# Turning a conv output to tokens by channels: four TensorE transposes per tile, or VectorE's 32x32 block transposes and a trip through DRAM

## The chip, the cores and the metric

The kernel runs on one core of one Trainium2 chip. The metric is the device time of one execution in microseconds (us), the median of several runs. Engines are named as the profile names them: PE (TensorE, the matrix engine; PEld is its weight load), DVE (VectorE), ACT (ScalarE), POOL (GpSimd) and SP (SyncE, which here only issues DMAs; SPq is its queue).

## What is computed

A decoder layer in float32 on 512 tokens (2 batches of 256) of 512 channels: a state-space mixer, a quantised product with a context, and a feed-forward with mixed experts. Nearly all of the time goes to the mixer. Cut to what matters here:

```python
proj = einsum('bsd,od->bso', h, in_proj_w)        # gate (8192), hBC (8192+2048), dt (128)
hBC  = silu(causal_conv(hBC, conv_w, conv_b))     # 4 taps per channel
hid, B, C = split(hBC)                            # hid: 128 heads of 64 channels
hid_dt = hid * dt[..., None]                      # dt: one value per token and head
y = sum over earlier tokens j of (C_i . B_j) * decay(i, j, head) * hid_dt[j]   # plus Dp * hid
y = y * silu(gate)                                # then an RMS norm over groups of 1024 channels
out = einsum('bsd,od->bso', y * rstd * gnorm_w, out_proj_w)
```

The projection makes hid with channels on the partitions (128 channels by 512 tokens), which the convolution wants. The sum over earlier tokens contracts over tokens, so it wants hid with tokens on the partitions, each value multiplied by dt of its token and head. Something has to turn hid round.

## The kernel before

**Tiles and steps.** The 8192 channels are 64 tiles of 128 channels (two heads each), in 8 groups g of 8. The main loop (L975) makes one step per tile, and one more per group for the tile of B and C of the next group ("state"), so 9 steps q = 0 to 8 in a group; the state has q = 4. It is a software pipeline: in one step, `z` is the tile being projected, `z1` the tile of the step before, `z2` the tile before that. On PE, ACT, DVE and POOL the instructions run in the order in which the program writes them; only the order of SP's DMAs is left to the scheduler of the framework, which places each by its own estimate of when it is ready.

**What one step does,** in program order:

- PE `begin(z)`: from group 1 on a product in seven block products instead of eight (L298); four of them come first. SP loads the weights (L342) and the decays of coming tiles (L457); POOL sums weights (L352 to L355).
- ACT starts z1's convolution out of PSUM (L313); then `times_dt(z2)` (L480): eight multiplications, one per block of 128 tokens and head, from PSUM tile `pht` to SBUF tile `hc`; then z1's gate (L427), and two copies out of `begin(z)`'s PSUM (`copy_first`, L386 and L387).
- For each of z1's two heads: DVE scans the decays (L487), ACT multiplies two blocks of them (L491), POOL multiplies by the inner products C.B into `mT` (L497). Between the two heads, DVE adds the other three taps of z1's convolution (L318), ACT takes its silu into `hid` (L321), and DVE combines `begin(z)`'s parts (`sum_begun`, L395 to L398).
- At q = 2 the norm of the group before: PE transposes the sum of squares (L537), DVE reduces it (L539), POOL computes the reciprocal root (L41 to L51) and then sums for the output product (L578 to L606).
- `seventh`: one block product of the output projection of an earlier group (L631), at q = 0, 2, 4, 5, 6, 7 ahead of the heads, at q = 1 behind everything (so "late"). In the last group there is one at q = 8 as well and a whole one at q = 3.
- `finish(pair)`: when two tiles z2 are ready, at q = 1, 3, 5 and 8 (one tile per step in the first group), PE multiplies `mT` by `hc` (`heads`, L508), and `gated` follows: DVE (L520, L523), ACT's square into `sq` (L528) and its scaling into `yw` (L530), POOL's sum of squares (L529).
- PE `complete(z)`: the remaining three block products.
- `by_tokens(z1)`: four PE transposes of `hid` against the identity into PSUM tile `pht` (L469). `times_dt` of the next step reads it.

So a tile's hid leaves the silu in one step, is turned at that step's end, is multiplied by dt at the start of the next step, and meets `heads` in that next step at the earliest. `conv` sums have a tile of their own (tag conv, 2 buffers), `y` has one buffer, `hc` two, `hid` three, the decays `dec` five, the weights `w` four.

Of the kernel before, what the change touches and what calls it, by code (L numbers as in the profile page):

```python
# [7 lines left out]
F32 = mybir.dt.float32  # L8
AF = mybir.ActivationFunctionType
ALU = mybir.AluOpType  # L10
# [3 lines left out]
P = 128  # L14
NB = 2
NT = 4
T = NT * P
S = T // NB
D = 512
KD = D // P  # L20
NG = 8
GJ = 8
HD = 64
# [12 lines left out]
def power(nc, pool, var, n, name):  # L36

    r0 = pool.tile([P, n], F32, tag="rs_r0", name=f"r0_{name}")
    ex = pool.tile([P, n], F32, tag="rs_ex", name=f"ex_{name}")
    nc.gpsimd.memset(ex[:], -0.5)  # L40
    nc.gpsimd.tensor_tensor(r0[:], var, ex[:], ALU.pow)  # L41
    return r0


def newton(engine, pool, out, r0, var, n, name):

    t0 = pool.tile([P, n], F32, tag="rs_t0", name=f"t0_{name}")
    engine.tensor_tensor(t0[:], r0[:], r0[:], ALU.mult)
    engine.tensor_tensor(t0[:], t0[:], var, ALU.mult)
    engine.tensor_scalar(t0[:], t0[:], -0.5, 1.5, ALU.mult, ALU.add)  # L50
    engine.tensor_tensor(out, r0[:], t0[:], ALU.mult)  # L51
# [3 lines left out]
def kernel(  # L55
# [25 lines left out]
    nc = tc.nc  # L81
# [14 lines left out]
    ident = const.tile([P, P], F32, name="ident")  # L96
# [5 lines left out]
    cw = const.tile([P, 80, 4], F32, name="cw")  # L102
    cb = const.tile([P, 80], F32, name="cb")
    ncw = const.tile([P, NG, 4], F32, name="ncw")
    gw = const.tile([P, NG * GJ], F32, name="gw")
# [4 lines left out]
    dt = const.tile([P, NT, P], F32, name="dt")  # L110


    dram = ctx.enter_context(tc.tile_pool(name="scratch", bufs=1, space=bass.MemoryType.DRAM))
# [5 lines left out]
    ps_y = main.enter_context(tc.tile_pool(name="ps_y", bufs=1, space=PSUM))  # L119
    ps_misc = main.enter_context(tc.tile_pool(name="ps_misc", bufs=1, space=PSUM))  # L120
    ps_seed = main.enter_context(tc.tile_pool(name="ps_seed", bufs=1, space=PSUM))
    ps_out = main.enter_context(tc.tile_pool(name="ps_out", bufs=1, space=PSUM))
    pool = main.enter_context(tc.tile_pool(name="main", bufs=2))
# [16 lines left out]

    with ExitStack() as first:
        pro = first.enter_context(tc.tile_pool(name="pro", bufs=1))
        wdt = pool.tile([P, KD, P], F32, tag="conv", name="wdt")
        nc.sync.dma_start(out=wdt[:], in_=in_w[DT0])
        for to, of in ((dtb, dt_bias.rearrange("(h o) -> h o", o=1)), (alog, a_log.rearrange("(h o) -> h o", o=1))):
            nc.sync.dma_start(out=to[:], in_=of)
# [39 lines left out]
        for b in range(NB):  # L186
# [16 lines left out]
        soft0, soft1, soft2 = (  # L203
            wpool.tile([P, 4 * T], F32, tag="wo", name=f"soft_{n}", bufs=3) for n in range(3)
        )
# [8 lines left out]
        nc.vector.tensor_tensor(v, v, u, ALU.subtract)  # L214
        nc.vector.tensor_tensor(dth, v, lg, ALU.add)
        nc.scalar.activation(within, dth, AF.Exp, scale=nega[:])
        zeros = pro.tile([P, P], F32, name="zeros")
        nc.gpsimd.memset(zeros[:], 0.0)
        for b in range(NB):
            nc.vector.tensor_tensor_scan(  # L220
                across[:, b * P : (b + 1) * P],
                within[:, (2 * b + 1) * P : (2 * b + 2) * P],
                zeros[:],
                1.0,
                ALU.mult,
                ALU.add,
            )
# [12 lines left out]
    def residual(n):  # L240

        if n == 0:
            res["var"] = small.tile([P, NT], F32, name="vare", bufs=1)
            nc.vector.tensor_scalar(res["var"][:], mv[:, :, 1], 1e-5, None, ALU.add)
            res["r0"] = power(nc, small, res["var"][:], NT, "l0")
        elif n == 1:
            res["rstd"] = small.tile([P, NT], F32, name="rstd_l0", bufs=1)
            newton(nc.gpsimd, small, res["rstd"][:], res["r0"], res["var"][:], NT, "l0")
        else:
            t = n - 2  # L250
            x1 = pool.tile([P, D], F32, tag="conv", name=f"x1_{t}")
            nc.vector.tensor_scalar(
                x1[:], acc[:, t, :], mv[:, t, 0:1], res["rstd"][:, t : t + 1], ALU.subtract, ALU.mult
            )
            nc.gpsimd.tensor_tensor(acc[:, t, :], acc[:, t, :], x1[:], ALU.add)
# [44 lines left out]
    def by_batch(ap):  # L300
        return ap.rearrange("p (b s) -> p b s", b=NB)

    class Conv:

        def __init__(self, dst, pvs, w, c, name):
            self.dst, self.w = dst, w
            self.a = pool.tile([P, T], F32, tag="conv", name=f"conv_{name}")
            av, n = by_batch(self.a[:]), NB // len(pvs)  # L310
            self.parts = [(av[:, i * n : (i + 1) * n], pv) for i, pv in enumerate(pvs)]
            for a, pv in self.parts:
                nc.scalar.activation(a, pv, AF.Identity, bias=cb[:, c : c + 1], scale=w[:, 3:4])  # L313
# [75 lines left out]
    def sum_begun(z):  # L389


        if not z.plain:
            z.g1 = pool.tile([P, S], F32, tag="g1", name=f"g1_{z.name}")[:]
            u = z.first[:, 0]
            nc.vector.tensor_tensor(u, z.all, u, ALU.subtract)  # L395
            nc.vector.tensor_tensor(z.h1, z.h1, u, ALU.subtract)
            nc.vector.tensor_tensor(z.g1, z.h1, z.first[:, 1], ALU.add)
            nc.vector.tensor_tensor(z.g0, z.g0, u, ALU.subtract)  # L398
# [7 lines left out]
    def start_conv(z):  # L406
        if isinstance(z, Tile):
            z.hid = pool.tile([P, T], F32, tag="hid", name=f"hid_{z.c}", bufs=3)
            z.convs = [Conv(z.hid[:], [by_batch(z.xy[0])], cw[:, z.c], z.c, f"h_{z.c}")]
            return  # L410
        g = z.g
        z.sT = [pool.tile([P, T], F32, tag=f"{n}T", name=f"{n}T_{g}", bufs=1) for n in "bc"]
        z.convs = [Conv(z.sT[0][:], [by_batch(z.xy[0])], cw[:, 64 + g], 64 + g, f"b_{g}")]
        if z.plain:
            pvs, w = [by_batch(z.xy[1])], cw[:, 72 + g]
        else:

            pvs, w = [a.unsqueeze(1) for a in (z.g0, z.g1)], ncw[:, g]
        z.convs.append(Conv(z.sT[1][:], pvs, w, 72 + g, f"c_{g}"))

    def gates(z, half):
        if half == 0:
# [36 lines left out]
            decs.append(dec)  # L459
        return decs  # L460

    def by_tokens(z, bank):

        c = z.c

        ps, tag = ((ps_misc, "misc"), (ps_y, "py"))[bank]
        pht = ps.tile([P, NT, 2, HD], F32, tag=tag, name=f"pht_{c}")
        for t in range(NT):
            nc.tensor.transpose(  # L469
                pht[:, t].rearrange("p h d -> p (h d)"), z.hid[:, t * P : (t + 1) * P], ident[:]  # L470
            )
        z.pht = pht

    def times_dt(z):
        c, pht = z.c, z.pht
        z.hc = pool.tile([P, NT, 2, HD], F32, tag="hc", name=f"hc_{c}", bufs=2)
        for t in range(NT):
            for n in range(2):
                h = 2 * c + n
                nc.scalar.mul(z.hc[:, t, n], pht[:, t, n], dt[:, t, h : h + 1])  # L480

    def decayed(z, n):

# [32 lines left out]
    def gated(z, sqsum, yw):  # L516

        c, hid, gate, py = z.c, z.hid, z.gate, z.py
        y = pool.tile([P, T], F32, tag="y", name=f"y_{c}", bufs=1)
        nc.vector.scalar_tensor_tensor(  # L520
            py[:], hid[:], dsk[:, c : c + 1], py[:], ALU.mult, ALU.add
        )
        nc.vector.tensor_tensor(y[:], py[:], gate[:], ALU.mult)  # L523
        if c % GJ == 0:
            nc.scalar.activation(sqsum[:], y[:], AF.Square)
        else:
            sq = pool.tile([P, T], F32, tag="sq", name=f"sq_{c}", bufs=2)
            nc.scalar.activation(sq[:], y[:], AF.Square)  # L528
            nc.gpsimd.tensor_tensor(sqsum[:], sqsum[:], sq[:], ALU.add)  # L529
        nc.scalar.mul(yw, y[:], gw[:, c : c + 1])  # L530

    def norm(o):

# [271 lines left out]
    rows = [Rows(t) for t in range(NT)]  # L805
# [161 lines left out]
    pair = []  # L967
# [7 lines left out]
    for s, (g, q, z) in enumerate(order):  # L975
        z1, z2 = (order[s - n][2] if s >= n else None for n in (1, 2))
        tile1 = isinstance(z1, Tile)
        c = g * GJ + q - (q > BC) if q != BC or g == NG else None
# [7 lines left out]
        n, part = divmod(s - GJ - 5, GT)  # L986
# [3 lines left out]
            next(part_of_context)  # L990
        if z1:
            start_conv(z1)
        if isinstance(z2, Tile):
            times_dt(z2)
        if tile1:
            gates(z1, 0)
        if z:
# [8 lines left out]
        if z1:  # L1006
            if tile1:
                gates(z1, 1)
            z1.convs[0].finish()
        if z:  # L1010
            sum_begun(z)
        if z1 and not tile1:
            z1.convs[1].finish()
            state = z1
# [47 lines left out]
        if isinstance(z2, Tile):  # L1062
            pair.append(z2)
        done = len(pair) == 2 or len(pair) == 1 and g in (0, NG)
        free = 0
        if done:
            free = 1 - len(pair) % 2 * (1 - pair[0].c % 2)
            finish(pair)
            pair = []
        if z:  # L1070
            complete(z)
        if tile1:
            by_tokens(z1, free)
        if late and next(going[0], True):
            going.pop()
        if 2 <= s < 2 + 2 + NT:
            residual(s - 2)
# [23 lines left out]
    add_out(last_o, 3)  # L1101
    rows[3].stats("l1")
    for t in range(2):
        rows[t].transpose("l1", "hc", 2)
    for t in range(2, NT):
        rows[t].scaled("l1", rsc[:, 0:1])
    for t in range(2, NT):
# [8 lines left out]
    for t in range(2):  # L1116
        rows[t].scaled("l2", None)
    for t in range(2, NT):
        rows[t].transpose("l1", "hc", 2)
    context(2)  # L1120
    add_context(2)
    rows[2].stats("l2")
# [78 lines left out]
```

## Time and profile before

| what | value |
| --- | --- |
| median of 3 runs | 847.02 us (846.75 to 847.85) |
| span of the profiled execution, first to last instruction | 846.3 us |
| busy: PE / PEld | 837.8 us / 651.8 us |
| busy: DVE / ACT / POOL | 628.7 / 478.8 / 656.0 us |
| L469, the transposes on PE: count, mean of one record | 256, 274 ns |
| L480, ACT times dt: count, mean of one record | 512, 332 ns |
| DMA: bytes, packets, share of 16 engines | 116.26 MB, 54953, 41.1% for SP's queue |

The page gives no time of the profiled execution but its span, which is 0.7 us under the median of the runs. A record's mean is from its start to its end; matmuls and ACT instructions overlap the next one, so a row of n of them takes less than n times the mean (four PE transposes take 0.44 us on the chain, eight multiplications of L480 1.75 us). Idle time of an engine is put down to what ended it.

### The profile page before, as it was taken

To read this page: it belongs to the slowest core of one execution; us is meant where nothing else is said; L and a number is where in the kernel's file an instruction comes from. 1 tells how busy PE (TensorE), PEld (TensorE's weight loads), DVE (VectorE), ACT (ScalarE), POOL (GpSimd) and SP (SyncE) were. 2 spreads that over 40 slices of the span, in tenths; PEclk is the share of its full clock that TensorE was granted. 3 is DMA by queue.
4 is the path that set the end of the run, shared out by engine and by line. 5 is a ranking of instruction groups with operands and counts; after the bars stand their busy time and mean duration, and the time that the engine had idled before them with its cause. 6 is when DMAs were issued, how large, how long until landed. Compare 5 with 4: busy or idle time off the path is not lost.

```text
span 846.3 us, 13509 instructions
## 1 busy us (share of the span) xinstructions
PE 837.8 (99%) x4368; PEld 651.8 (77%) x4368; DVE 628.7 (74%) x1031; ACT 478.8 (57%) x1362; POOL 656.0 (78%) x675
## 2 busy tenths in 40 slices
PE   8999999999999999999999999999999999999998
PEld 6444578888888888888888888888888888885453
DVE  5667578788779778787779778788778786885663
ACT  2566576556664666556674666557664565655130
POOL 2156689998799888998799888998799888984210
PEclk9999999999999999999999999999999999999999
DMA  6684434346434363255433463235542473323001
GB/s 175 207 295 131 143 125 134 103 150 217 136 123 136 127 223 125 79 183 177 165 132 110 149 228 113 75 125 155 184 138 72 139 245 98 116 88 124 1 1 50
DMA packets 54953, 116.26 MB, mean 137 GB/s; under 512 B 7746, under 2 KB 8002, under 8 KB 54883
## 3 DMA queue, kind: packets, MB, share of 16 engines
q1 hardware_dynamic: 54882, 115.40, 41.1%
q8 instruction: 35, 0.57, 0.3%
q14 instruction: 36, 0.29, 0.1%
HBM read 111.84 MB, written 3.54 MB: 136 GB/s over the span
## 4 chain that ended last, share of the span: by engine, by line
PE 81%; POOL 11%; ACT 3%; DVE 2%; issue 2%; DMA 1%; SPq 0%; POOLq 0%; DVEq 0%; ACTq 0%
PE x L298 18%; PE m L631 17%; PE y L298 13%; PE py L508 9%; PE x L292 4%; PE y L292 4%; PE po L688 3%; PE pht L469 3%; POOL mT L497 3%; POOL t L593 2%; POOL yw L584 2%; POOL wo L598 2%; PE pf L803 2%; PE pq L803 2%; PE x_bc L298 1%
## 5 line engine op out<-in xcount | busy, mean ns | idle before, releaser
L497 POOL TENSOR_TENSOR mT<-lT,inner 128x768 f32<-128x768 f32 x128 | 232.6, 1819 | 79.0 <-ACT lT L491 78.5
L318 DVE SCALAR_TENSOR_TENSOR conv_h<-x,cw,conv_h 128x510 f32<-128x510 f32 (+2 forms) x192 | 142.7, 743 | 41.4 <-ACT conv_h L313 36.5
L631 PE MATMUL m<-wo,yw 128*128 128x256 f32 x672 | 155.1, 381 | 0.6
L487 DVE TENSOR_TENSOR_SCAN lT<-dec,seed 128x512 f32<-128x512 f32 x128 | 154.2, 1210 | 0.0
L631 PEld LDWEIGHTS m<-wo,yw 128*128 128x128 f32 x672 | 125.1, 190 | 20.0 <-POOL wo L598 4.3
L491 ACT ACTIVATE lT<-dec,lT 128x128 f32<-128x128 f32 x256 | 90.3, 408 | 86.7 <-DVE lT L487 85.1
L480 ACT ACTIVATE hc<-pht,dt 128x64 f32<-128x64 f32 x512 | 111.6, 332 | 10.9 <-PE pht L469 10.9
L298 PE MATMUL x<-hT,w 128*128 128x256 f32 x440 | 116.6, 387 | 0.0
L298 PE MATMUL y<-hs,w 128*128 128x256 f32 x440 | 112.0, 379 | 0.0
L529 POOL TENSOR_TENSOR sqsum<-sqsum,sq 128x512 f32<-128x512 f32 x56 | 73.1, 1305 | 29.3 <-ACT sq L528 26.5
L298 PEld LDWEIGHTS x<-hT,w 128*128 128x128 f32 x440 | 80.5, 190 | 16.7 <-issue 5.0
L508 PE MATMUL py<-mT,hc 128*64 128x256 f32 (+1 forms) x1024 | 91.2, 329 | 0.6 <-ACT inner L449 0.6
L508 PEld LDWEIGHTS py<-mT,hc 128*64 128x64 f32 x1024 | 64.3, 137 | 31.7 <-issue 9.1
L298 PEld LDWEIGHTS y<-hs,w 128*128 128x128 f32 x440 | 80.3, 190 | 9.2
L528 ACT ACTIVATE sq<-y 128x512 f32<-128x512 f32 x56 | 35.4, 632 | 65.9 <-DVE y L523 65.9
L520 DVE SCALAR_TENSOR_TENSOR py<-hid,dsk,py 128x512 f32<-128x512 f32 x64 | 47.6, 743 | 27.8 <-PE py L508 27.8
L395 DVE TENSOR_TENSOR first<-y,first 128x256 f32<-128x256 f32 x55 | 23.3, 424 | 52.9 <-ACT first L387 52.0
L313 ACT ACTIVATE conv_h<-x,cb,cw 128x512 f32<-128x512 f32 x64 | 49.2, 769 | 18.8 <-PE x L298 18.8
L523 DVE TENSOR_TENSOR y<-py,gate 128x512 f32<-128x512 f32 x64 | 44.3, 692 | 19.4 <-ACT yw L530 18.2
L298 PE MATMUL y<-hs,ws 128*128 128x256 f32 x220 | 56.5, 379 | 0.0
L298 PE MATMUL x<-hT,ws 128*128 128x256 f32 x220 | 56.5, 379 | 0.0
L298 PE MATMUL x<-hs,ws 128*128 128x256 f32 x220 | 56.5, 379 | 0.0
(239 smaller groups left out, 1465.2 us busy)
## 6 DMA issues: line engine op xcount, KB each, us to landing
dec<-decays SPq DMA_DIRECT2D x128, 384.0 KB, 3.5
w<-in_in_w SPq DMA_DIRECT2D x128, 256.0 KB, 3.1
wo<-in_out_w SPq DMA_DIRECT2D x16, 1024.0 KB, 7.2
w_bc<-in_in_w SPq DMA_DIRECT2D x16, 256.0 KB, 5.2
kvin<-in_ctx_kv SPq DMA_DIRECT2D x4, 512.0 KB, 4.7
kvq<-kvin SPq DMA_DIRECT2D x4, 512.0 KB, 2.8
kv<-kvq SPq DMA_DIRECT2D x4, 512.0 KB, 3.5
acc<-in_x SPq DMA_DIRECT2D x4, 256.0 KB, 3.9
```

What stands on the lines that cost most here:

```text
L292: nc.tensor.matmul(pp, w[:, k, :], hT[:, k, :], start=(k == 0), stop=(k == KD - 1))
L298: nc.tensor.matmul(out, w[:, k, :], h[:, k, :], start=clear and k == 0, stop=(k == KD // 2 - 1), skip_group_check=True)
L313: nc.scalar.activation(a, pv, AF.Identity, bias=cb[:, c : c + 1], scale=w[:, 3:4])
L318: nc.vector.scalar_tensor_tensor(a[:, :, d:], pv[:, :, : S - d], self.w[:, 3 - d : 4 - d], a[:, :, d:], ALU.mult, ALU.add)
L480: nc.scalar.mul(z.hc[:, t, n], pht[:, t, n], dt[:, t, h : h + 1])
L487: nc.vector.tensor_tensor_scan(lT[:, 0:NT, :].rearrange("p t i -> p (t i)"), dec[:, 0:T], seed[:], 0.0, ALU.mult, ALU.add)
L491: nc.scalar.mul(lT[:, NT + b, :], dec[:, T + b * P : T + (b + 1) * P], lT[:, 2 * b, P - 1 : P])
L497: nc.gpsimd.tensor_tensor(m[:], z.lT[n][:], inner[:], ALU.mult)
L508: nc.tensor.matmul(z.py[n * HD : (n + 1) * HD, b * S + s * P : (b + 1) * S], z.hc[:, 2 * b + s, n, :], z.mT[n][:, part, :], start=(s == 0) ...
L520: nc.vector.scalar_tensor_tensor(py[:], hid[:], dsk[:, c : c + 1], py[:], ALU.mult, ALU.add)
L529: nc.gpsimd.tensor_tensor(sqsum[:], sqsum[:], sq[:], ALU.add)
L631: nc.tensor.matmul(o.po[:, t, :], lhs[k][:, t * P : (t + 1) * P], rhs[k], start=(k == 0), stop=(k == GJ // 2 - 1))
```

## The change

`by_tokens` no longer uses PE. DVE transposes hid within blocks of 32 by 32 into an SBUF tile `blocks`; SP writes its four partition quarters to a DRAM scratch tile `swap`, each block to its turned place, in pieces of 32 floats (128 bytes), and then reads the scratch back into `hc` with tokens on the partitions, in pieces of 128 floats. `times_dt` multiplies `hc` in place, SBUF to SBUF. `by_tokens` moves from the end of the step to just behind `sum_begun`, `times_dt` from ahead of the gate to behind the silu of z1. The convolution's sums are made in `hid` itself (for the state in a `hid` and a `conv` buffer), `y` is squared in place after its scaling, and buffer counts follow: `hc` 3, `y` 2, `conv` 1, no `sq`. The 128x128 zeros of the prologue become a slice of another tile.

```diff
-            z.convs = [Conv(z.hid[:], [by_batch(z.xy[0])], cw[:, z.c], z.c, f"h_{z.c}")]
+            z.convs = [Conv(z.hid[:], [by_batch(z.xy[0])], cw[:, z.c], z.c, z.hid)]
...
+        sums = [pool.tile([P, T], F32, tag=n, name=f"{n}_bc_{g}", bufs=b) for n, b in (("hid", 3), ("conv", 1))]
...
-    def by_tokens(z, bank):
-        ps, tag = ((ps_misc, "misc"), (ps_y, "py"))[bank]
-        pht = ps.tile([P, NT, 2, HD], F32, tag=tag, name=f"pht_{c}")
-        for t in range(NT):
-            nc.tensor.transpose(
-                pht[:, t].rearrange("p h d -> p (h d)"), z.hid[:, t * P : (t + 1) * P], ident[:]
-            )
-        z.pht = pht
+    def by_tokens(z):
+        blocks = pool.tile([P, NT * 4, 32], F32, tag="blocks", name=f"blocks_{z.c}", bufs=1)
+        nc.vector.transpose(blocks[:].rearrange("p k c -> p (k c)"), z.hid[:])
+        swap = dram.tile([NT, P, P], F32, tag="swap", name=f"swap_{z.c}", bufs=3)
+        to = swap[:].rearrange("t (b r) (a c) -> a r (t b) c", r=32, c=32)
+        for a in range(4):
+            nc.sync.dma_start(out=to[a], in_=blocks[32 * a : 32 * a + 32])
+        z.hc = pool.tile([P, NT, 2, HD], F32, tag="hc", name=f"hc_{z.c}", bufs=3)
+        nc.sync.dma_start(
+            out=z.hc[:].rearrange("p t h d -> p t (h d)"), in_=swap[:].rearrange("t p c -> p t c")
+        )
 
     def times_dt(z):
...
-                nc.scalar.mul(z.hc[:, t, n], pht[:, t, n], dt[:, t, h : h + 1])
+                nc.scalar.mul(z.hc[:, t, n], z.hc[:, t, n], dt[:, t, h : h + 1])
...
-        y = pool.tile([P, T], F32, tag="y", name=f"y_{c}", bufs=1)
+        y = pool.tile([P, T], F32, tag="y", name=f"y_{c}", bufs=2)
...
+        nc.scalar.mul(yw, y[:], gw[:, c : c + 1])
         if c % GJ == 0:
             nc.scalar.activation(sqsum[:], y[:], AF.Square)
         else:
-            sq = pool.tile([P, T], F32, tag="sq", name=f"sq_{c}", bufs=2)
-            nc.scalar.activation(sq[:], y[:], AF.Square)
-            nc.gpsimd.tensor_tensor(sqsum[:], sqsum[:], sq[:], ALU.add)
-        nc.scalar.mul(yw, y[:], gw[:, c : c + 1])
+            nc.scalar.activation(y[:], y[:], AF.Square)
+            nc.gpsimd.tensor_tensor(sqsum[:], sqsum[:], y[:], ALU.add)
...
         if z1:
             start_conv(z1)
-        if isinstance(z2, Tile):
-            times_dt(z2)
         if tile1:
             gates(z1, 0)
...
             z1.convs[0].finish()
+        if isinstance(z2, Tile):
+            times_dt(z2)
         if z:
             sum_begun(z)
+        if tile1:
+            by_tokens(z1)
...
-        if tile1:
-            by_tokens(z1, free)
```

More of the change, by code (lines that the diff above doesn't have):

```diff
@@ L142 @@
         pro = first.enter_context(tc.tile_pool(name="pro", bufs=1))
-        wdt = pool.tile([P, KD, P], F32, tag="conv", name="wdt")
+        wdt = pool.tile([P, KD, P], F32, tag="conv", name="wdt", bufs=1)
         nc.sync.dma_start(out=wdt[:], in_=in_w[DT0])
@@ L216 @@
         nc.scalar.activation(within, dth, AF.Exp, scale=nega[:])
-        zeros = pro.tile([P, P], F32, name="zeros")
-        nc.gpsimd.memset(zeros[:], 0.0)
+        zeros = soft2[:, T : T + P]
+        nc.gpsimd.memset(zeros, 0.0)
         for b in range(NB):
@@ L222 @@
                 within[:, (2 * b + 1) * P : (2 * b + 2) * P],
-                zeros[:],
+                zeros,
                 1.0,
@@ L250, in residual @@
             t = n - 2
-            x1 = pool.tile([P, D], F32, tag="conv", name=f"x1_{t}")
+            x1 = pool.tile([P, D], F32, tag="conv", name=f"x1_{t}", bufs=1)
             nc.vector.tensor_scalar(
@@ L303, with __init__ @@
     class Conv:
-        def __init__(self, dst, pvs, w, c, name):
-            self.dst, self.w = dst, w
-            self.a = pool.tile([P, T], F32, tag="conv", name=f"conv_{name}")
+        def __init__(self, dst, pvs, w, c, a):
+            self.dst, self.w, self.a = dst, w, a
             av, n = by_batch(self.a[:]), NB // len(pvs)
@@ L412, in start_conv @@
         z.sT = [pool.tile([P, T], F32, tag=f"{n}T", name=f"{n}T_{g}", bufs=1) for n in "bc"]
-        z.convs = [Conv(z.sT[0][:], [by_batch(z.xy[0])], cw[:, 64 + g], 64 + g, f"b_{g}")]
+        sums = [pool.tile([P, T], F32, tag=n, name=f"{n}_bc_{g}", bufs=b) for n, b in (("hid", 3), ("conv", 1))]
+        z.convs = [Conv(z.sT[0][:], [by_batch(z.xy[0])], cw[:, 64 + g], 64 + g, sums[0])]
         if z.plain:
@@ L418, in start_conv @@
             pvs, w = [a.unsqueeze(1) for a in (z.g0, z.g1)], ncw[:, g]
-        z.convs.append(Conv(z.sT[1][:], pvs, w, 72 + g, f"c_{g}"))
+        z.convs.append(Conv(z.sT[1][:], pvs, w, 72 + g, sums[1]))
     def gates(z, half):
@@ L460, in load_decays @@
         return decs
-    def by_tokens(z, bank):
-        c = z.c
-        ps, tag = ((ps_misc, "misc"), (ps_y, "py"))[bank]
-        pht = ps.tile([P, NT, 2, HD], F32, tag=tag, name=f"pht_{c}")
-        for t in range(NT):
-            nc.tensor.transpose(
-                pht[:, t].rearrange("p h d -> p (h d)"), z.hid[:, t * P : (t + 1) * P], ident[:]
-            )
-        z.pht = pht
+    def by_tokens(z):
[9 more added lines that the diff above has]
+        )
     def times_dt(z):
-        c, pht = z.c, z.pht
-        z.hc = pool.tile([P, NT, 2, HD], F32, tag="hc", name=f"hc_{c}", bufs=2)
         for t in range(NT):
             for n in range(2):
-                h = 2 * c + n
-                nc.scalar.mul(z.hc[:, t, n], pht[:, t, n], dt[:, t, h : h + 1])
+                h = 2 * z.c + n
+                nc.scalar.mul(z.hc[:, t, n], z.hc[:, t, n], dt[:, t, h : h + 1])
     def decayed(z, n):
@@ L1064 @@
         done = len(pair) == 2 or len(pair) == 1 and g in (0, NG)
-        free = 0
         if done:
-            free = 1 - len(pair) % 2 * (1 - pair[0].c % 2)
             finish(pair)
@@ L1103 @@
     for t in range(2):
-        rows[t].transpose("l1", "hc", 2)
+        rows[t].transpose("l1", "hc", 3)
     for t in range(2, NT):
@@ L1118 @@
     for t in range(2, NT):
-        rows[t].transpose("l1", "hc", 2)
+        rows[t].transpose("l1", "hc", 3)
     context(2)
```

## The prediction, made before the changed kernel was run

> **What bounds the kernel now.** I read the page's busy times and chain first, then the busy time by stage, then the chain and the engines' instructions inside two steps.
>
> ```profile
> PE 837.8 (99%) x4368; PEld 651.8 (77%) x4368; DVE 628.7 (74%) x1031; ACT 478.8 (57%) x1362; POOL 656.0 (78%) x675
> PE 81%; POOL 11%; ACT 3%; DVE 2%; issue 2%; DMA 1%; SPq 0%; POOLq 0%; DVEq 0%; ACTq 0%
> ```
>
> By stage (columns: PE, PEld, DVE, ACT, POOL busy, PE clock, DMA share, GB/s), nine steps take about 95 us:
>
> ```profile
> 310.00:405.00 95.00, 94.90 (x536) 80.33 (x535) 75.01 (x119) 58.72 (x170) 86.02 (x89) 1.00 0.45 147
> 405.00:500.00 95.00, 94.90 (x532) 80.54 (x532) 74.94 (x119) 59.33 (x171) 85.87 (x89) 1.00 0.42 143
> ```
>
> PE never rests, at full clock, so PE sets the end. But POOL is 90% busy and DVE 79%: take 3.5 us of PE from a group, and POOL has 86 us of work in 91.5. The chain through a step with q = 8 shows PE's order (start, duration):
>
> ```profile
> 474.23 0.44 PE pht L469 x4
> 474.67 1.73 PE y L298 x8
> 476.40 1.73 PE x L298 x8
> 478.13 0.45 PE pcr L448 x4
> 478.57 2.75 PE py L508 x32
> ```
>
> and ACT in that step:
>
> ```profile
> 474.71 1.75 ACT L480 ACTIVATE hc<-pht,dt 128x64 f32<-128x64 f32 x8 [0.52 <-PE pht L469]
> ...
> 478.16 0.37 ACT L387 COPY first<-x 128x256 f32<-128x256 f32 x1 [1.17 <-PE x L298]
> 478.61 0.37 ACT L449 COPY inner<-pcr 128x256 f32<-128x256 f32 x1
> 478.88 0.69 ACT L491 ACTIVATE lT<-dec,lT 128x128 f32<-128x128 f32 x2
> 479.47 0.40 ACT L427 ACTIVATE gate<-g 128x256 f32<-128x256 f32 x1
> 479.78 0.62 ACT L321 ACTIVATE hid<-conv_h 128x512 f32<-128x512 f32 x1
> ```
>
> The turned hid is ready at 474.7, `hc` at 476.5, and the heads read it from 478.57: two microseconds to spare. ACT's next stretch is released by PE's own first products and ends at 480.4.
>
> **What is removed.** 64 tiles of four transposes at 0.44 us on the chain: 64 x 0.44 = **-28.2 us**, if PE stays the bound.
>
> **times_dt behind the silu.** On ACT the eight multiplications now start where the silu ends: 480.3 in the step above. Their pace from SBUF: L491, SBUF to SBUF, starts one every 0.29 us at 128 columns; less 64 columns (about 0.05) 0.24, against 0.20 from PSUM. Eight take 0.33 + 7 x 0.24 = 2.0 us, to 482.3, and PE's last pair of products after them 0.2. The heads of the pair begin at 478.57 with the older tile, ready since the step before, and take 2.75 us, to 481.32. So PE stops for about 1.2 us (1.0 at PSUM's pace, 1.9 at eight whole records of 332 ns). The same holds at q = 1, where heads follow `begin` at once (silu to 499.77, heads 497.94 to 500.69). At q = 3 and q = 5 output products go ahead of the heads; the multiplications end 0.4 us early at q = 3, and free. In group 0 `begin` is long enough (silu to 63.4, multiplications to 65.3, heads of one tile to 65.5). With 7 steps of q = 1 (groups 1 to 7) and 6 of q = 8 (in group 7 an output product is ahead), 13 x 1.2 = **+15.6 us**. Queued behind the moved multiplications on ACT are L491 of z1's second head, 0.8 us later than now, and POOL's `mT`, which the heads want a step later at the earliest: free.
>
> **DVE's block transpose.** No row has one. Below it 0.40 us (L267 does 1024 columns in 0.80), above it the scan's 1.21 for 512 columns; I take 0.70, nearest to L523's 692 ns for the same tile. DVE has 20 us idle in 95, so 9 x 0.7 fit; but it waits for the silu, and behind it on DVE stand, at q = 2, the norm's reduction (L539) and so POOL's chain. There POOL works without a pause from the reduction to the sums of `wo`, and PE is already at their end:
>
> ```profile
> PEld m L631 <- POOL wo L598: 4.3, 12, 0.5
> ```
>
> PE waits there 0.6 us in each of 7 groups. After the change PE comes two transposes (0.88) earlier, POOL 0.7 later: 7 x 1.58 = **+11.1 us** (7 x 1.28 with the short transpose, 7 x 2.1 with the long). Removing L480 from ACT doesn't start that chain sooner: the copy L387 ahead of it is released by PE.
>
> **The trip through DRAM.** It must fit between the silu of one step and that of the next. SP's five issues take 0.33 to 0.57 us each, say 0.42. No row writes 128-byte pieces; the nearest transfers:
>
> ```profile
> dec<-decays SPq DMA_DIRECT2D x128, 384.0 KB, 3.5
> w<-in_in_w SPq DMA_DIRECT2D x128, 256.0 KB, 3.1
> decays<-soft SPq DMA_DIRECT2D x1, 256.0 KB, 2.2
> fa<-in_ffn_a SPq DMA_DIRECT2D x1, 64.0 KB, 2.2
> ```
>
> fa is 64 KB in 128-byte pieces, as each quarter is, but read. A trip: semaphore 0.1, four issues 1.7, landing of the last 2.3 (from 1.7 for the smaller write to decays to 2.8 for kvq), the read 3.1 as w (2.2 to 6.8, dec's longest): 7.2 us. It adds 131,072 short pieces and 32,768 of 512 bytes to 54,953 packets. What a short piece costs a DMA engine at least shows in a stretch of mostly 32-byte pieces: 0.2 us x 16 x 0.53 for 6.6 KB, or 206 pieces, 8 ns each.
>
> ```profile
> 25.60:25.80 0.20, 0.20 (x1) 0.01 (x1) 0.00 (x0) 0.00 (x0) 0.00 (x0) 1.00 0.53 33
> ```
>
> At most I take what 512 bytes cost at the full rate, 22 ns (338 GB/s at share 0.93). A tile's 2048 pieces are then 1.0 to 2.8 us of all 16 engines, its read 0.7; a step's present 4.5 us become 6.2 to 8.0 of 10.3. With rings that full I add 1.0 us of waiting: **8.2 us**. In the changed program's SP order the loads of `dec` and `w` stand between writes and read; they wait for L491 and PE products of the same step, about when the writes land. Weights are loaded several tiles ahead, so their delay is free.
>
> Against the need, on the old clock, less 0.44 for the shorter step: from q = 7 to 8, transpose done 471.0, landed 479.2, needed 479.9: fits. From q = 0 to 1: done 490.7, landed 498.9, needed 499.2, but a 1 MB load of `wo` (7.2 us to landing) goes ahead of the read and costs some 1.5: late 1.2, 7 x 1.2 = **+8.4 us**. From q = 2 to 3 it is late by 0.6, inside the wait for POOL just counted. In group 0 late by 0.5: 7 x 0.5 = **+3.5 us**.
>
> The Trainium skill ("DMA: Bandwidth & Descriptors", Specifications) speaks against the trip: below 512 bytes a transfer becomes a read-modify-write. No run here has yet shown a short write. If each piece cost two passes of 512 bytes, an estimate from that rule and the full-rate row, the writes would take 5.6 us, the trip would grow by 2.8 and the sum by some 55 us.
>
> **Edits at nothing.** The convolution in `hid`: its buffer, three back, is last read by L520 at 452.6, over 2 us before the conv at 455.2 that reuses it. The square in place comes 0.7 us later and `sqsum` with it; the norm's transposes read that 4 us after POOL has it (506.7, 510.7). A second `y` frees DVE of 0.65 us waits (18.2 us in all), none on the chain. If one of these covers goes, the cost is below 1 us per group.
>
> **The sum.** 846.3 - 28.2 + 15.6 + 11.1 + 8.4 + 3.5 = 856.7 us of span; with the 0.7 us by which the median stands over it, **857.4**. What can be told from no change is about 0.2%, 1.7 us.
>
> **The rivals.**
>
> - The trip fits everywhere, and the multiplications go at PSUM's pace: 846.3 - 28.2 + 13 x 1.0 + 7 x 1.28 + 0.7 = 840.8; without POOL's wait 831.8. **Faster**, chance 0.23. For it: DMA engines idle 55%, the trip's slack is within my 1.0 us. Against: PE's order at q = 1 and 8 fixes the stall even with an early landing. It decides when the trip is below about 7 us.
> - The terms cancel: POOL at 90% or a shorter trip gives back what PE saves, 847, chance 0.12. For it: four terms of 4 to 16 us against 28.
> - Short writes are slow, and every tile waits for its `hc`. Beyond 8.2 us each further microsecond costs 7 (q = 1), 6 (q = 8, after 0.7) and 7 (group 0), 20 us in all. With four issues of 0.57, landings of 2.8 and 6.8 the trip is 12: 857.4 + 3.8 x 20 = 930. At 10 us, about 890. Chance 0.20 for over 870.
> - The forecast, 849 to 870: chance 0.45.
>
> Faster 0.23, same 0.12, slower 0.65. The range goes from 838 (trip fits, POOL's wait at its small end) to 890 (trip of 10 us), with about 0.1 left out on either side.
>
> **What would show it.** Right: no L469 on PE; PE waits for ACT's L480 instructions at the heads of q = 1 and 8 by about 1.2 us and at no other; L631 waits for POOL about 2 us per group; block transposes of about 0.7 us; `hc` landing 3 us after its issue; DMA share 0.55 to 0.75. Wrong: ACT idle before the multiplications for a DMA in every step (the trip is too slow), or heads without waits (the multiplications come early enough), or DVE as what PE's `complete` waits for.

## The result and the profile after

The changed kernel takes 925.71 us (median of 4 runs, 923.75 to 926.28), against 847.4 us for the kernel before on the same chip: 1.092 times as long, 95% interval 1.0905 to 1.0935. The prediction was 857.4 us with a range from 838 to 890. The profiled execution took 926.09 us with a span of 924.0. From the page after: the busy times, the chain by engine, and the DMA queue of SP (packets, MB, share of 16 engines):

```profile
PE 848.6 (92%) x4112; PEld 656.9 (71%) x4112; DVE 672.3 (73%) x1095; ACT 506.9 (55%) x1362; POOL 655.2 (71%) x675
PE 63%; DMA 18%; DVE 7%; ACT 6%; issue 3%; SPq 2%; POOL 1%; DVEq 0%; ACTq 0%; POOLq 0%
q1 hardware_dynamic: 223842, 148.98, 59.2%
```

PE lost its 256 transposes (4368 to 4112 instructions) and yet is busy for longer than before, and idle for 75.4 us in place of 8.5. The chain, which was PE with POOL, now has 18% of transfers. By stage, nine steps (columns as before: length, then PE, PEld, DVE, ACT, POOL busy, PE clock, DMA share, GB/s):

```profile
342.20:447.10 104.90, 96.89 (x508) 81.89 (x508) 82.51 (x130) 62.78 (x172) 86.53 (x89) 0.97 0.65 178
```

A group takes 105 us in place of 96 (the prediction's windows of 95 us are a little short of a group), PE rests 8 us of them, and its clock is 0.97, not 1.00. POOL is busy for as long as before (86.5 us of a group), ACT for 62.8 us in place of 59.4, and DVE, which has the block transposes now, for 82.5 in place of 76.3. What PE waits for, from the waits (total us, times, longest), and the landings of the transfers (KB each, median us from issue to landing):

```profile
ACT hc L479 <- DMA hc<-swap: 75.4, 27, 4.5
PE py L507 <- ACT hc L479: 60.9, 20, 5.6
swap<-blocks SPq DMA_DIRECT2D x256, 64.0 KB, 2.8
hc<-swap SPq DMA_DIRECT2D x64, 256.0 KB, 4.4
L465 DVE STREAM_TRANSPOSE blocks<-hid 128x512 f32<-128x512 f32 x64 | 45.1, 704 | 10.5 <-ACT hid L320 9.9
```

The heads (L507) wait for the multiplications by dt, and these for the read of the scratch. The block transpose itself takes 0.70 us, as predicted. In groups 1 to 6 PE stops for `hc` at three heads: at q = 1 and q = 3 for 3.0 to 5.6 us, at q = 8 for 0.7 to 1.8 us. At q = 8 four of the six stops are 0.71 us long, which is the stop that run 2 keeps without any transfer (below), so the trip itself is late there in group 4 and hardly elsewhere. One more stop, of 3.90 us, is for a load of `wo` at the end (847.64).

**Where the trip is long.** The chain through the trip that ends at q = 1 (start, duration):

```profile
434.38 0.71 DVE blocks L465
...
435.10 0.32 SPq L469
...
436.67 2.56 DMA swap<-blocks
...
439.24 7.46 DMA hc<-swap
...
446.72 0.36 ACT hc L479
```

From the transpose's end (435.09) to the landing (446.70) are 11.6 us. The writes land at 439.23, as early as predicted; the read alone takes 7.46 us. SP issued 384 KB of decays at 437.27 and a 1 MB load of `wo` at 437.80, between the writes and the read. The trip that ends at q = 3 shows another cause, in SP's queue:

```profile
463.30 1.96 SPq L469 DMA_DIRECT2D swap<-blocks  x4
465.93 4.18 SPq L457 DMA_DIRECT2D dec<-decays  x2
470.29 0.37 SPq L471 DMA_DIRECT2D hc<-swap  x1
```

The read is not issued before 470.29, 5 us after the last write. Ahead of it stand two loads of decays that wait for their buffers; the chain shows SP released at 470.06 by ACT's gate instruction. The read lands at 474.68, 11.4 us after the transpose. The trip that ends at q = 8 of the same group takes 10.0 us (519.92 to 529.88), the last 6.27 of them in the read.

### The profile page after: what moved, and what is told of

Its sections match the earlier page's. It is cut to its first block, busy times and chain, and to the rows that moved or that the text cites. A ratio compares the mean times of both kernels' runs of the same rounds, so it can differ in the third digit from the quotient of the medians.

```text
span 924.0 us, 13482 instructions
## 1 busy us (share of the span) xinstructions
PE 848.6 (92%) x4112; PEld 656.9 (71%) x4112; DVE 672.3 (73%) x1095; ACT 506.9 (55%) x1362; POOL 655.2 (71%) x675
## 4 chain that ended last, share of the span: by engine, by line
PE 63%; DMA 18%; DVE 7%; ACT 6%; issue 3%; SPq 2%; POOL 1%; DVEq 0%; ACTq 0%; POOLq 0%
PE x L298 15%; PE m L629 11%; DMA hc<-swap 11%; PE y L298 10%; PE py L507 9%; DMA swap<-blocks 3%; PE x L292 3%; PE po L686 2%; PE x_bc L298 2%; PE y L292 2%; ACT lT L490 2%; DVE hid L317 2%; PE y_bc L298 2%; SPq L469 2%; PE pf L801 2%
## 5 line engine op out<-in xcount | busy, mean ns | idle before, releaser
L317 DVE SCALAR_TENSOR_TENSOR hid<-x,cw,hid 128x510 f32<-128x510 f32 (+2 forms) x192 | 142.6, 743 | 60.8 <-ACT hid L312 56.2
L507 PE MATMUL py<-mT,hc 128*64 128x256 f32 (+1 forms) x1024 | 121.5, 371 | 65.1 <-ACT hc L479 60.9
L479 ACT ACTIVATE hc<-hc,dt 128x64 f32<-128x64 f32 x512 | 128.8, 335 | 75.5 <-DMA hc<-swap 75.4
L507 PEld LDWEIGHTS py<-mT,hc 128*64 128x64 f32 x1024 | 87.2, 151 | 102.2 <-issue 54.6
L298 PE MATMUL y<-hs,w 128*128 128x256 f32 x440 | 106.2, 379 | 0.0
L528 POOL TENSOR_TENSOR sqsum<-sqsum,y 128x512 f32<-128x512 f32 x56 | 74.1, 1323 | 43.8 <-ACT y L527 42.4
L523 ACT ACTIVATE yw<-y,gw 128x512 f32<-128x512 f32 x64 | 46.0, 719 | 51.1 <-DVE y L522 50.7
L386 ACT COPY first<-x 128x256 f32<-128x256 f32 x55 | 20.5, 372 | 70.8 <-PE x L298 70.8
L312 ACT ACTIVATE hid<-x,cb,cw 128x512 f32<-128x512 f32 x64 | 49.1, 768 | 9.3 <-PE x L298 9.3
L465 DVE STREAM_TRANSPOSE blocks<-hid 128x512 f32<-128x512 f32 x64 | 45.1, 704 | 10.5 <-ACT hid L320 9.9
```

What stands on the lines that cost most here:

```text
L298: nc.tensor.matmul(out, w[:, k, :], h[:, k, :], start=clear and k == 0, stop=(k == KD // 2 - 1), skip_group_check=True)
L317: nc.vector.scalar_tensor_tensor(a[:, :, d:], pv[:, :, : S - d], self.w[:, 3 - d : 4 - d], a[:, :, d:], ALU.mult, ALU.add)
L479: nc.scalar.mul(z.hc[:, t, n], z.hc[:, t, n], dt[:, t, h : h + 1])
L507: nc.tensor.matmul(z.py[n * HD : (n + 1) * HD, b * S + s * P : (b + 1) * S], z.hc[:, 2 * b + s, n, :], z.mT[n][:, part, :], start=(s == 0) ...
L528: nc.gpsimd.tensor_tensor(sqsum[:], sqsum[:], y[:], ALU.add)
```

## The experiments

The first reading of the two traces gave theory L (late trip) and two rivals: R (the added traffic delays the loads of weights and decays) and S (the new places of the work on DVE and ACT, and the edits in place).

**1. No wait for the trip.** The trip's DMAs stay, but `hc` no longer comes out of them.

```diff
-        z.hc = pool.tile([P, NT, 2, HD], F32, tag="hc", name=f"hc_{z.c}", bufs=3)
+        got = pool.tile([P, NT, 2, HD], F32, tag="got", name=f"got_{z.c}", bufs=1)
...
-                nc.scalar.mul(z.hc[:, t, n], z.hc[:, t, n], dt[:, t, h : h + 1])
+                nc.scalar.mul(z.hc[:, t, n], hid[:, t, n], dt[:, t, h : h + 1])
```

> This kernel keeps the transposes on VectorE, the writes to the scratch and the reads from it, but the reads go to a tile that nobody uses, and the multiplication by dt takes its input from hid as it stands, channels by tokens, so that nothing waits for the trip; with that its output is not the reference's. Theory L (the trip comes late, behind the loads in the rings, and what TensorE lost at a slower clock follows from these stops): 832 to 848 us, idle time of TensorE near 25 us, granted clock back over 0.99. Rival R (the added traffic delays the weights and decays): over 870, with stops behind the loads of w and dec. Rival S (the new place of the multiplication by dt, the transposes on VectorE and the edits in place cost most): over 870 with stops behind VectorE or ScalarE.

Measured: 903.80 us. L's range is missed by 56 us. PE now waits for `wo`:

```profile
437.68 4.34 PE L631 MATMUL m<-wo,yw 128*128 128x256 f32 x12 [4.04 <-DMA wo<-in_out_w]
```

**2. No transfers of the trip at all.** `by_tokens` ends behind the block transpose.

> As the run without the wait, and the scratch's writes and reads are left out as well (output not the reference's); the transposes on VectorE stay. L: within 4 us of the run that keeps the transfers, 830 to 848. R: this run alone is fast, by 20 us or more. S: over 870, like the run that keeps the transfers.

Measured: 854.64 us (ratio 1.0084, 1.0069 to 1.0099). By the expectations that is R, with 49 us for the transfers. Run 9 shows that these two runs differ in more than that.

**3. The read on ScalarE's queue.** `nc.sync` becomes `nc.scalar` for the read, issued behind `start_conv(z1)`.

> The changed kernel with one edit: the read of hc is issued from ScalarE's DMA queue, behind the first instruction of the next tile's convolution, in place of SyncE's queue, where it stands behind the loads of decays and weights. The output is the reference's. L: the read lands 1.5 to 3 us sooner against the loads, hc comes in time for most tiles, 860 to 895 us. R and S: 915 us or more, since neither the bytes nor the order of the engines' work changes much.

Measured: 937.27 us, worse than the change. ACT works in program order, and now it stood still for the writes to land:

```profile
ACT gate L427 <- DMA swap<-blocks: 32.1, 14, 6.5
```

**4. The edits in place alone,** in the kernel before.

> The kernel before with only the edits that the prediction costed at nothing: the convolution in hid itself, y squared in place behind its multiplication by gw, and the number of buffers; the transposes stay on TensorE. L and R: 847 plus or minus 1.7 us. S: part of the 78 us lost, that is 855 us or more.

Measured: 847.95 us, ratio 1.0006 (0.9997 to 1.0015): they cost nothing that can be measured.

**5. The same transfers, free of waits.** To split R: is it the waits in SP's queue (Q) or the pieces (P)?

```diff
-            nc.sync.dma_start(out=to[a], in_=blocks[32 * a : 32 * a + 32])
+            nc.sync.dma_start(out=to[a], in_=hT[32 * a : 32 * a + 32, 0].rearrange("r (k c) -> r k c", c=32))
...
-            ..., in_=swap[:].rearrange("t p c -> p t c")
+            ..., in_=swaps[max(len(swaps) - 4, 0)][:].rearrange("t p c -> p t c")
```

> As the run without the wait for hc (903.8 us), with as many transfers of the same pieces and bytes at the same places of the program, but none of them waits for work of the same tile: the writes take their data from hT, which is constant, and the reads fetch a scratch written three tiles earlier. The output is not the reference's. Two theories for the 49 us between the runs with and without the trip's transfers. Q (SyncE's queue is one line: a write that waits for its transpose, or a read that waits for its writes, holds back the loads of weights, decays and wo queued behind it): back to 853 to 868 us. P (pieces of 128 B and fuller rings make the loads themselves land later): 890 us or more.

**6. Long pieces.** Run 1 with `to = swap[:].rearrange("t (r u) c -> t r (u c)", u=4)`, so that each write fills one stretch.

> As the run without the wait for hc (903.8 us), all waits of the trip kept, but each write puts 2 KB pieces in one stretch of the scratch, in place of 128 B pieces (65,536 B per write as before); the output is not the reference's. Q: 885 to 905 us, since the waits in SyncE's queue stay, at most 1 us shorter each. P: 855 to 870 us.

Measured: 906.82 us without waits, 855.52 us with long pieces. Both speak for P, but there was a flaw in all four: the scheduler had laid SP's queue in a different order in each. In run 1 a group's first load of `wo` is issued at 430.67, 2.7 us after PE went on with the heads of q = 1 (427.98); in run 6 at 497.98, 9.1 us ahead of that point (507.06). The other engines' orders are the same in runs 1, 2, 5 and 6.

**7. The multiplication by dt at its old place,** in run 2's kernel.

> As the run without any transfer of the trip (854.6 us), with the multiplication by dt at its old place, behind the first instruction of the next convolution; the output is not the reference's. If the prediction's term for the later place is right (13 stops of 1.2 us, 15.6 us): 836 to 843 us. If the place costs nothing: 852 us or more.

Measured: 840.86 us, so the later place costs 13.8 us (predicted 15.6).

**8. The whole trip on ScalarE's queue,** writes and read.

> The changed kernel with the whole trip on ScalarE's DMA queue: the four writes where they stood in the program, the read ahead of the next step's copies of the first sums. The output is the reference's. Q: SyncE's loads are as early as in the kernel before, TensorE loses only what ScalarE's issues (five of 0.4 to 0.5 us a tile) and a late hc cost: 865 to 905 us. P: 915 us or more, as many bytes in as small pieces.

Measured: 932.96 us. It fails as run 3 did; ACT waits 44.2 us for the writes to land ahead of L385. So this run tells nothing on Q or P.

**9. Run 1 with the queue order of run 6.** Each of the loop's 608 SP DMAs is chained behind the one ahead of it in a written list; the chain sets the order of issue and adds no wait for an end.

```diff
+    queue = [sent[k[0]][int(k[1:])] for k in QUEUE.split()]
+    for a, b in zip(queue, queue[1:]):
+        tc.add_manual_dep(
+            b, a.name, mybir.DependencyInfo(mybir.DependencyClass.NoSync, mybir.DependencyReason.DATA), reason="queue"
+        )
```

> As the run without the wait for hc (903.8 us), with its short pieces and all its waits, and with one thing changed: SyncE's instructions stand in the order that the scheduler gave the run with the 2 KB pieces (855.5 us); the orders of the other four engines are the same in all three. The output is not the reference's. O (the 49 us come from the order in which the scheduler, which counts short pieces as dear, queued the loads, so that the first load of wo stands 12 us later): 853 to 862 us. P (they come from the short pieces in the rings): 895 us or more. In between: shared.

Measured: 860.98 us. So 42.8 of the 48.3 us between runs 1 and 6 are the order. PE waits for `wo` no more (but once, at the end), and what is left is the structure that the prediction had counted:

```profile
441.21 4.09 PE L638 MATMUL m<-wo,yw 128*128 128x256 f32 x16 [0.85 <-POOL wo L605]
486.28 2.06 PE L516 MATMUL py<-mT,hc 128*64 128x256 f32 x16 [0.71 <-issue]
506.28 2.02 PE L516 MATMUL py<-mT,hc 128*64 128x256 f32 x16 [0.76 <-ACT hc L488]
```

The 5.5 us left are not shown to be the short pieces. PE makes the product `pcr` (L448 in the kernel before) once in each of these groups, at q = 8; its starts (us) give the length of a group:

| run | in group 1 | in group 6 | one group |
| --- | --- | --- | --- |
| before | 188.89 | 670.32 | 96.29 |
| 7, no transfers, multiplication early | 190.99 | 665.39 | 94.88 |
| 2, no transfers | 192.96 | 678.29 | 97.07 |
| 6, 2 KB pieces in the writes | 193.07 | 678.43 | 97.07 |
| 9, 128 B pieces | 192.32 | 677.62 | 97.06 |
| after | 213.07 | 738.22 | 105.03 |

A group is as long in run 9 as in runs 2 and 6. The difference is the one stop at the end, with slower products behind it:

```profile
774.93 0.34 SPq L755 DMA_DIRECT2D kv<-kvq  x1
775.38 0.39 SPq L576 DMA_DIRECT2D wo<-in_out_w  x1
782.29 3.75 PE L695 MATMUL po<-wo,yw 128*128 128x512 f32 x4 [3.95 <-DMA wo<-in_out_w]
```

The chain does not hold the loads for the context. In run 9 one of them, `kv`, stands ahead of this load of `wo` and waits 2.3 us for a product of PE; in run 6 it stands behind, and the same `wo` is issued at 772.00. The four writes ahead of both are issued in 3.58 us in run 9 and in 2.04 in run 6. So order and pieces both have a hand in this stop, and no run separates them.

R and P, then, were for the most part artefacts of order: without the wait for `hc`, and in a good order, the whole trip costs 6.3 us over run 2, and nothing that shows in a group of the loop.

**10. The changed kernel in that order** (the same chain, nothing else).

> The changed kernel, wait for hc and all, with that same order of SyncE's instructions. The output is the reference's. If the order of the loads is the whole loss beyond the prediction: 857 to 870 us. If the late trip is a loss of its own (loads of decays and weights still stand between the writes and the read of 59 of 64 tiles): 885 to 915 us. If the pieces are the cause: 920 us or more.

Measured: 903.63 us (1.0635 to 1.0671 times before), in the range for a late trip. Against run 9 the only difference that bears on time is that `hc` comes out of the read: 42.7 us for waiting. Against the changed kernel it gains 22.1. Its late trip at q = 1 (in a profiled execution of 910.31 us):

```profile
429.23 6.05 DMA swap<-blocks
...
435.40 4.46 DMA hc<-swap
```

Here 1 MB of `wo` was issued ahead of the writes, at 426.26, and it is the writes that land late, 6.05 us after the last one's issue began.

**11. The read straight behind the writes,** in the changed kernel's own order; what stood between goes behind the read.

> The changed kernel with SyncE's own order of it, but for one thing: what stood between a tile's last write and its read (a load of decays and one of weights for most tiles, a load of wo for seven) is put straight behind the read. The output is the reference's. L (the read comes late because it stands behind 640 KB or more in the queue and rings): hc is in time for most tiles, 855 to 885 us. If the loads, which now wait for the writes to land, become the late ones: 900 us or more, with TensorE waiting for w or wo in place of hc.

Measured: 889.22 us, a gain of 36.5: L's mechanism, and 4 us short of its range. In groups 2 to 6 the heads of q = 1 are back at the stop of 0.71 us that comes of the structure. The read lands sooner, and SP pays for it by waiting for the writes:

```profile
hc<-swap SPq DMA_DIRECT2D x64, 256.0 KB, 3.0
SPq L478 <- DMA swap<-blocks: 156.0, 96, 4.3
449.76 2.61 PE L514 MATMUL py<-mT,hc 128*64 128x256 f32 x16 [3.37 <-ACT hc L486]
```

The last line is what remains: one late `hc` a group, at q = 3 (3.4 to 4.0 us in groups 2 to 5, 1.1 in group 6), and single ones in the first and the last groups.

**12. Runs 10 and 11 together.**

> The changed kernel with the order of SyncE's loads that gave 903.6 us, and with what stands between a tile's last write and its read put straight behind the read. The output is the reference's. If both gains add (22 us from the order of the loads, 36 us from the read straight behind the writes, partly the same thing): 862 to 882 us. If the second replaces the first: 885 to 892 us.

Measured: 903.22 us. Neither expectation holds. In run 6's order a load of `wo` stands ahead of the writes whose tile is needed at q = 1, and pulling the read forward does nothing for late writes: 4.0 to 4.9 us of stop there in groups 2 to 5 and 7, 2.3 in group 6.

**13 and 14. Long pieces in the changed kernel,** in run 10's order: in the writes, then in the read too.

> The changed kernel with the order of SyncE's instructions of the 903.6 us run, and the four writes of a tile in 2 KB pieces instead of 128 B ones, as many bytes, into a scratch in the wrong order (so the output is not the reference's); the read and the wait for it stay. If the short pieces make the trip late: 862 to 880 us. If its place among the loads does: 890 to 905 us.

> As the run with 2 KB pieces in the writes, and the read in 2 KB pieces too instead of 512 B ones (output not the reference's). If pieces are what counts, a few us below that run, 858 to 875. If the place among the loads is: within 5 us of it and over 885.

Measured: 877.65 and 876.80 us; the second lies in neither of its ranges. So pieces and place are both causes. Against run 10 the long pieces in the writes gain 26.0 us. Some 6 of these are the stop at the end again: run 10 has it (4.01 us, `kv` ahead of `wo`), and run 13, in which all of SP's transfers, `kv` too, are in run 6's order, has none. The other 20 are left to the short pieces, where PE waits for `hc`; where nothing waited for them (run 9) they did not lengthen a group. The 512 B pieces of the read cost nothing that these runs resolve. The landing of a write falls from 2.7 to 2.1 us. The late places stay, but short:

```profile
502.87 2.06 PE L514 MATMUL py<-mT,hc 128*64 128x256 f32 x16 [1.32 <-ACT hc L486]
523.85 2.06 PE L514 MATMUL py<-mT,hc 128*64 128x256 f32 x16 [1.73 <-ACT hc L486]
```

**15. Three loads moved from ahead of the writes to behind the read,** in run 11's kernel, in five groups.

> The run with the read straight behind the writes (889.2 us), and in groups 2 to 6 two loads of weights and the 1 MB load of wo, which stood ahead of the writes of the tile whose heads come at q = 3, put behind that tile's read. The output is the reference's. If these loads in the rings make the trip late: each of five stops of 3.4 to 3.6 us at q = 3 shrinks to 1 us or less, with the slow products behind it, 3 us each, so 870 to 877 us. If short pieces alone make it late: 886 us or more. If the moved loads now come late themselves: 886 us or more, with stops at wo or at w in place of hc.

Measured: 880.60 us (878.33 to 885.6). The stop for `hc` at q = 3 is gone in these groups. The gain is 8.6 us, not the 12 or more expected, because POOL comes next: at the same heads PE waits 0.6 to 1.4 us for POOL's `mT`, and behind them for POOL's sums of `wo`:

```profile
447.94 1.51 PE L514 MATMUL py<-mT,hc 128*64 128x256 f32 x14 [1.43 <-POOL mT L503]
456.54 4.09 PE L636 MATMUL m<-wo,yw 128*128 128x256 f32 x16 [0.85 <-POOL wo L603]
```

This is the best kernel with the whole trip. With the engines' work in this order it can hardly fall below run 2's 854.6 us, which has no transfer at all, and that is above 847. Only the early multiplication (840.9) is below, and for it the trip would have to end before the next step's first products; that wasn't tried.

**The whole difference, step by step,** from the medians:

| from | to | us | what |
| --- | --- | --- | --- |
| before 847.5 | run 7, 840.9 | -6.6 | transposes off PE, block transposes on DVE |
| run 7 | run 2, 854.6 | +13.8 | multiplication by dt behind the silu |
| run 2 | run 6, 855.5 | +0.9 | the trip's transfers, 2 KB pieces in the writes |
| run 6 | run 9, 861.0 | +5.5 | 128 B pieces and a `kv` load ahead of `wo`: one stop at the end |
| run 9 | run 10, 903.6 | +42.7 | waiting for the read |
| run 10 | after, 925.7 | +22.1 | the scheduler's own order of SP's queue |

## Why the prediction was wrong

The side was right, and PE remained the engine that sets the end (63% of the chain); the time was 68 us too low and outside the range.

- **-28.2 for the transposes.** PE has 256 instructions fewer, but run 7 gains 6.6 us, not 28. In a group eight tiles of transposes are 3.5 us, and run 7's group is 1.41 us shorter: PE is busy for 93.55 us in place of 96.24, which is 2.69 less, and idle for 1.23 more. Of the idle time 0.86 is the wait for POOL's sums of `wo` at q = 2, which the prediction had counted (**+11.1**). It is smaller: 0.86 in 6 groups, 5.2 us. The 4.3 us that the prediction read there are waits of PEld, the weight load; PE had no stop there before, only 4.07 us for 16 products that elsewhere take 3.62, and they take 4.09 now. Another 2.8 us in all are waits for DVE's `sum_begun`. Some 6 us are in the first two groups, which the prediction did not have: in run 7 stops of 2.27 (for POOL) and 2.60 (for ACT's `inner`) and slower products behind them. The rest, 0.8 us a group, is products that take longer without a stop; why is open.
- **+15.6 for times_dt behind the silu.** Right: 13.8 by medians. In run 9's trace a stop of 0.71 and 2.06 in place of 1.52 for the 16 products behind it, 1.25 us, at 12 heads; the prediction had 13 of 1.2.
- **Edits at nothing** (run 4) and **DVE's transpose of 0.70** (0.704): right. Without its two trip terms (8.4 and 3.5) the prediction's sum is 846.3 - 28.2 + 15.6 + 11.1 + 0.7 = 845.5; run 2, without the trip, measured 854.6. A group was forecast well: 96.29 - 3.52 + 2 x 1.2 + 1.58 = 96.75 us, and run 2 has 97.07. But at q = 8 of group 1 run 2 is 4.1 us behind the kernel before, where the same terms would have it some 3.5 us ahead; so 7 to 8 of the 9 us lie in the first two groups.
- **The trip of 8.2 us: the step that failed.** The prediction said: "With rings that full I add 1.0 us of waiting: **8.2 us**. In the changed program's SP order the loads of `dec` and `w` stand between writes and read; they wait for L491 and PE products of the same step, about when the writes land." Its single pieces were right: issues 2.0 us (1.7), writes landed 2.0 to 2.8 us after the last issue began (2.3), and a read behind nothing lands in 3.0 (3.1, run 11). But the trips that PE waits for take 11.6, 11.4 and 10.0 us (group 4). At q = 3 the decays' buffers come free 5 us after the writes are issued, not "about when the writes land", and the read stands behind them; the stops there, which it put at nothing ("inside the wait for POOL"), are 3.1 to 3.5 us. At q = 1 the 1 MB load and the 384 KB of decays ahead of the read cost 4.4 us of landing (7.46 against 3.0), not 1.5. Run 11 shows this by taking just these loads from between writes and read: 36.5 us.
- **The late trip's price.** At 20 us for each microsecond of trip, the rival "every tile waits for its `hc`" gave 930 for a trip of 12. The three trips above are 11.0 us on average, which by that rule makes 857.4 + 2.8 x 20 = 913; measured 925.7. That this comes near is partly luck. The rule counts q = 1, q = 8 and group 0; but at q = 8 the stops hardly grew, q = 3, which it leaves out, lost over 3 us a group, and the sum has no term for products that run slower behind a stop: PE is busy for 21.7 us more than in run 9 (last section). Nor was the rival's cause, short writes that land slowly, the whole: long pieces gave back 26 us (run 13, against run 10), a better place in the queue 36 (run 11, against the changed kernel).
- **"Weights are loaded several tiles ahead, so their delay is free."** True of the changed kernel, whose PE waits for `hc`, but for the stop of 3.90 us at the end. In run 1, in another order, 12 us on the issue of `wo` cost 43 us.

The Trainium skill ("DMA: Bandwidth & Descriptors", Specifications) says that below 512 bytes a transfer is a read-modify-write; the prediction's estimate from that was 2.8 us more on the trip and 55 on the sum. The measured difference between 128 B and 2 KB pieces is 0.6 us in a write's landing (2.7 against 2.1) and 26 us on the sum, some 6 of them in the stop at the end: the rule stood on the right side, and the estimate from it was too high. Whether the cost comes of a read-modify-write no run here shows.

What stays open: how a short piece makes the trip longer (its own landing, or the time that what is queued ahead of it needs), its share in the stop at the end, and the products that take longer without a stop.

## What to carry to other kernels

A transfer on the critical path must be priced where it stands in its queue: list what is issued ahead of it and between its two halves, and for each of these the buffer that it waits for, since one load that waits for a buffer holds all behind it. When experiments remove or resize transfers and a scheduler lays the queue, compare the queue orders of the kernels first and pin one order, with every transfer in it, or the difference between two runs may be the order's: here a load outside the chain had a hand in 5.5 us. A fixed product that comes once per group shows in which stretch two runs differ. Work moved off the bounding engine can be worth much less than its time when the next engine is at 90%: here 6.6 us of 28 were left before any transfer was added, and 1.4 of 3.5 in a group, with 0.86 lost to POOL.

## What the runs showed of the hardware

**PE's clock falls after a stop.** The changed kernel's PE is busy for 848.6 us and run 9's for 826.9 with the same products: 22 of the 65 us between their spans (924.0 and 859.2). The mean granted clock is 0.962 in the one and 0.994 in the other. After the stop of 2.98 us that ends at 342.27 (columns as above):

```profile
341.00:342.00 1.00, 0.00 (x0) 0.00 (x0) 1.00 (x2) 0.18 (x1) 0.00 (x0) 1.00 0.82 229
342.00:343.00 1.00, 0.73 (x3) 0.55 (x5) 0.97 (x2) 1.00 (x5) 0.00 (x0) 0.71 0.97 212
343.00:344.00 1.00, 1.00 (x10) 0.99 (x8) 0.13 (x1) 1.00 (x5) 0.00 (x0) 0.50 0.82 128
344.00:345.00 1.00, 1.00 (x9) 0.55 (x5) 0.00 (x0) 1.00 (x3) 0.50 (x1) 0.50 0.92 218
345.00:346.00 1.00, 1.00 (x4) 0.65 (x3) 0.62 (x1) 0.67 (x2) 1.00 (x1) 0.58 0.55 163
```

The granted clock is 1.00 while PE stands still and about 0.50 for some 3 us once it works again (1.00 from 346.00 on); 16 products take 3.07 us in place of 2.06. Behind stops under 2 us these 16 products take 2.06. Of the longer stops most have such a stretch (2.7 to 3.1 us), but their length does not decide: one of 2.09 us (to 113.53, clock 0.50 behind it) has it, while one of 2.24 (to 101.87), one of 3.51 (to 238.60) and one of 3.28 us (to 763.59) have none, with the clock at 1.00. The Trainium skill ("TensorE: Matmul & The Clock Gate", Part 1) describes half rate after an idle window of about 3.4 us that runs free of the kernel, which fits the stretch and the exceptions; that stops of 2.98 and even 2.09 us were enough does not quite fit the window's length.

**Issues can stall without a wait.** Four write issues take 2.0 us as a median, but 5.05 us right behind a `wo` load (run 10) and up to 7.56 in run 5, with no semaphore named. With 2 KB pieces the longest four took 2.9 us (run 13) and 3.3 (run 6). The cause was not tried.
